# A planner's costs recounted in a four-layer graph network: landing times per kind of transfer, a microsecond in hand for each, and VectorE's pauses

## The chip, the cores and the metric

The kernel runs on one core of one Trainium2 chip. The metric is the device time of one execution in microseconds (us). Before the change the median of three runs is 2305.0 us (2304.22 to 2305.61). All arithmetic is in fp32.

## The reference

Thirty-two graphs of 512 nodes go through four layers. Each layer multiplies by the graph's 512 x 512 adjacency matrix, applies one or two dense products, adds the result to its input and normalises over the 256 features. The data of one graph never meets another's.

```python
def layernorm(x): return (x - mean(x)) / sqrt(var(x) + 1e-5)          # over the 256 features
# x: (32, 512, 256), adj: (32, 512, 512)
def L0(x): return relu(((1 + eps) * x + adj @ x) @ W1 + b1) @ W2 + b2     # 256 -> 512 -> 256
def L1(x): h = adj @ (x @ W.T + b); return where(h > 0, h, alpha * h)
def L2(x): h = layernorm(x); return x + relu((adj @ h) @ W_rel + b_rel + h @ W_root)
def L3(x):
    h = (epsilon * x + adj @ x) @ W1 + b1                                 # 256 -> 1024
    return silu(h * rsqrt(mean(h * h) + 1e-6) * rms_weight) @ W2 + b2     # 1024 -> 256
for L in (L0, L1, L2, L3):
    x = layernorm(x + L(x))
```

## The kernel before

**The work of a graph.** One graph's activations (512 x 256) fill one "room", an SBUF buffer of 128 partitions x 1024 floats; there are 36 rooms, and up to five graphs are under way at once (`FLIGHT`). An adjacency matrix fills two rooms and is loaded by four transfers of 256 KB; x is one transfer of 512 KB. Every large product is done as seven products of half size in place of eight, so VectorE makes many sums and differences of blocks before a product (`left_sums`, `right_sums`) and adds many PSUM results after it. ScalarE does the normalisations' sums and scalings, the activations and copies out of PSUM. GpSimd does only small powers (`inv_sqrt`).

**Transfers inside the core.** Where a tensor must be turned, VectorE transposes squares of 32 x 32 and SyncE's queue carries them through a buffer in device memory and back: four transfers of 128 KB out (`corner<-room` in the profile), then one of 512 KB or four of 128 KB back in (`room<-corner`). `spread_squares` and `gather_squares` do this in two layouts. The diagonal blocks of the adjacency are put aside and brought back in the same way (`diagonal`), and `everywhere` spreads one row over all partitions through `line`. `carry` moves four blocks from room to room, for the first graph alone.

**The order of the work.** The program's order is fixed when it is built. Each helper (`mm`, `add`, `copy`, `move` ...) only records an `Op` with, for each engine that could do it, a pair of times: how long the engine is busy, and how long after that the result is there. `Plan.order` then simulates the engines with these times and writes down the ops in the order in which they start; engines then run their own streams in this order, held only by semaphores. Line 332 issues nearly all compute instructions and line 372 all transfers.

What the simulation goes by:

- An op's **rank** is a due time: the graph's number times a period, plus a shift for single graphs (`SHIFT`), plus the TensorE work of its graph that lies before the product that needs it, times a pace, less the cost of the chain between (`needs`). `near` weighs that chain. The last three graphs (`LATE`) follow at a spacing of their own. Among ops that can start at the same moment on an engine, the lowest rank goes first. `RULES` holds period, pace, last spacing and `near`.
- `AHEAD` bounds how far, in units of rank, an op that takes a new room may be ahead of the foremost matmul that is still to do.
- A **transfer** occupies SyncE's queue for `ISSUE` and lands at the end of its turn on the wire (kbytes / 385) plus `ADVANCE` 1.5 us, plus `late` and `AFTER`. At most eight are under way (`LANES`). What reads the target can't start earlier in the simulation, and the room isn't free before.
- An op that both ScalarE and VectorE can do goes to VectorE only if it would end there `YIELD` us earlier.
- **Pauses.** A GpSimd power and VectorE instructions with two SBUF operands are kept apart (`port`). After VectorE has made a power's input, the next such instruction starts no earlier than `PORT` = 0.55 us later. If nothing else fits, the simulated idle time is stored as `op.pause`, and the emitter at line 1454 fills it with small memsets, one for each 0.11 us:

```python
if op.pause and op.way == "vector":
    for _ in range(round(op.pause / 0.11)):
        nc.vector.memset(pause, 0.0)
```

Of the kernel before, what the change touches and what calls it, by code (L numbers as in the profile page):

```python
# [14 lines left out]
P = 128  # L15
Q = 32
# [4 lines left out]
def span(ap):  # L21

    n = 1
    for d in ap.shape[1:]:
        n *= d
    return n
# [38 lines left out]

ISSUE, ADVANCE, AFTER, LANES = dict(sync=0.45, within=0.66, gpsimd=1.5), 1.5, 0.8, 8


def wire_time(kbytes):
    return kbytes / 385
# [19 lines left out]
SOON = 0.03  # L92


YIELD = 1.4

# [2 lines left out]

RULES = [(35, 1.8, 14, 0.8)]

SHIFT = {-2: -3, -1: -12}


AHEAD, LAST = 55.0, 500.0


TURN = {0: (99, 0), 2: (99, 0), 3: (0, 3)}
# [132 lines left out]
class Plan:  # L247
# [113 lines left out]
        ways = {"vector": ((busy, vector_time(1)[1]), issue)}  # L361
        self.add(ways, [s[0] for s in steps], ins, port=True, crosses=True)

    def move(self, out, src, kbytes, engine="sync", late=0.0, into=None, outof=(), **kw):


        within = engine == "sync" and isinstance(out, Part) and isinstance(src, Part)
        kind = "within" if within else engine

        def issue():  # L370
            to, of = (x.place() if isinstance(x, Part) else x for x in (out, src))
            getattr(self.nc, engine).dma_start(to, of, **kw)  # L372

        self.add(
            {engine: ((ISSUE[kind], ADVANCE + late + wire_time(kbytes) + AFTER), issue)},
            into or out, [*outof, *([src] if isinstance(src, Part) else [])],
            kbytes=kbytes, late=late,
        )
# [53 lines left out]
    def best(self):  # L432


        rule = min(RULES, key=lambda rule: self.order(*rule)[0])
        return self.order(*rule)[1]

    def order(self, period, pace, last, near):
# [4 lines left out]
        rank = [  # L443
            (min(op.graph, final) * period + max(op.graph - final, 0) * last + SHIFT.get(op.graph, 0) + SHIFT.get(op.graph - B, 0) + n, i)
            for i, (op, n) in enumerate(zip(self.ops, need))
# [11 lines left out]
        oldest, ahead, wire, lanes = 0, 0, 0.0, [0.0] * LANES  # L457
# [9 lines left out]
        while can_start:  # L467
# [50 lines left out]
            for i in can_start:  # L518
                op = self.ops[i]
# [6 lines left out]
                if op.kbytes and "sync" in op.ways:  # L526
# [4 lines left out]
                way = min(  # L531
                    at, key=lambda e: at[e] + sum(op.ways[e][0]) + YIELD * (op.yields and e == "vector")
                )
# [3 lines left out]
            t, engine = min((min(c)[0], e) for e, c in best.items())  # L537
            soon = t + (1e-6 if engine == "tensor" else SOON)
            _, t, i = min((r, s, i) for s, r, i in best[engine] if s <= soon)
            op = self.ops[i]  # L540
# [15 lines left out]
            end = t + busy + tail  # L556
# [6 lines left out]
                    port["vector"] = t + busy + PORT  # L563
            if op.kbytes:
                wire = max(wire, t + ADVANCE) + wire_time(op.kbytes)
                end = wire + op.late + AFTER
                if engine == "sync":
                    lanes = [*lanes[1:], end]
            for r in op.rooms:
# [27 lines left out]
def tile_gnn_stack(ctx: ExitStack, tc: tile.TileContext, a: dict, out: bass.AP):  # L597
# [26 lines left out]
    B, N, D = a["x"].shape  # L624
    NC = N // P
    DC = D // P
# [13 lines left out]
    plan = Plan(nc, FLIGHT)  # L640
# [31 lines left out]
    def vector(method, n, *args, **kw):  # L672
        return "vector", method, vector_time(n), args, kw

    def scalar(func, n, x, times=scalar_time, **kw):
        columns = sum(k in ("scale", "bias") and not isinstance(v, float) for k, v in kw.items())
        return "scalar", "activation", times(n, columns), (x,), dict(func=func, **kw)
# [34 lines left out]
        plan.do(o, way)  # L712

    def carry(o, x):
        plan.move(o, x, o.shape[0] * span(o) / 256, late=1.2)

    def inv_sqrt(o, x):
        n, p = span(o), o.shape[0]
# [5 lines left out]
    def room(*shape):  # L724
        return Part(Room(rooms)).shaped(*shape)
# [120 lines left out]
    class Adjacency:  # L846
# [35 lines left out]
        def restore(self):  # L882
            for i in range(4):
                if plan.graph == 0:
                    carry(self.loops[i], self.kept[:, i])
                elif i < 2:
                    for k in range(HC):
                        c = i * HC + k
                        block = a["adj"][plan.graph][:, c, c * P : (c + 1) * P]
                        plan.move(self.loops[i][:, k], block, P * P / 256)  # L890
                else:
                    name = f"{self.kept.tensor.name}{i}"
                    d = self.kept[:, i - 2]
                    plan.move(self.loops[i], d, P * HC * P / 256, outof=[name])
# [134 lines left out]
    def dense_turned(right, left, bias=None):  # L1029
# [27 lines left out]
        for k in range(DC):  # L1057
# [5 lines left out]
                ),  # L1063
            )
        y = spread_squares(squares)
        return y.whole(P // Q, NC, DC, Q).then(lambda v: v.rearrange("p a c k j -> p c k a j"))

# [34 lines left out]
    class Norm:  # L1102
# [44 lines left out]
        def put(self, c, y, scale, shift):  # L1147
            r = self.r[:, c, :]
            plan.do(
                y[:, c, :],  # L1150
                vector(
                    "tensor_scalar", D, r, self.less[:, c : c + 1], scale, op0=ALU.add, op1=ALU.mult
                ),
                scalar(AF.Identity, D, r, scale=scale, bias=shift),
            )
# [53 lines left out]
    def spread_squares(of):  # L1209

        to = room(P // Q, NC * DC * Q)
        of, via = of.whole(P // Q, NC * DC * Q), next(corners)
        names = [f"{via.tensor.name}{a}" for a in range(P // Q)]
        places = via.rearrange("(b i) (a x) -> a i b x", i=Q, a=P // Q)
        for a, name in enumerate(names):
            plan.move(places[a], of[a * Q : (a + 1) * Q], Q * N * DC / 256, into=name)
        plan.move(to.whole(N * DC), via, P * N * DC / 256, late=0.8, outof=names)
        return to  # L1220

    def gather_squares(to, of):

        to, of, via = to.whole(N * DC), of.whole(N * DC // Q, Q), next(corners)
        names = [f"{via.tensor.name}{a}" for a in range(P // Q)]
        via = via.rearrange("(i b) x -> i (b x)", i=Q)
        places = via.rearrange("i (m a j) -> a i m j", a=P // Q, j=Q)
        for a, name in enumerate(names):  # L1230
            plan.move(places[a], of[a * Q : (a + 1) * Q], Q * N * DC / 256, into=name)
        blocks = via.rearrange("i (b x) -> b i x", b=P // Q)
        for b in range(P // Q):
            plan.move(to[b * Q : (b + 1) * Q], blocks[b], Q * N * DC / 256, late=0.8, outof=names)

    def everywhere(sums, ops):

# [37 lines left out]
    def load_x(b):  # L1275
        x = tok()
        src = a["x"][b].rearrange("(p c) d -> p c d", c=NC)
        if b:
            plan.move(x, src, N * D / 256, late=1.6)
        else:  # L1280
            for h in range(2):
                plan.move(half(x, h), half(src, h), N * D / 512, late=1.6)
        return x

    def layer0(x, adjacency):
        adjacency.sums()
        adjacency.with_loops(loop0)
        aT = aggregate(x, adjacency)
        adjacency.restore()
        turn = turns(0)  # L1290
        if not turn:
            plus_row(x, b2_0)
        h1 = Wide(FC0)
        dense_feat(aT, A1_0, b1_0, h1, lambda f: act(h1.pair(f), h1.pair(f), AF.Relu))
        norm = Norm(x)
        right = dense_sums([halves(h1.pair(0))], [halves(h1.pair(2))])
        if turn:
            add_turned(x, dense_turned(right, A2_0, b2c_0), norm.half)
        else:
            dense_add(x, right, A2_0, norm.half)  # L1300
        norm.scales((1.0, LN_EPS))
        return norm.scaled()
# [104 lines left out]
    x = load_x(0)  # L1407
# [13 lines left out]
    x = layer0(x, adjacency)  # L1421
# [22 lines left out]
    for b in range(1, B):  # L1444
        plan.graph = b
        x, adjacency = load_x(b), Adjacency(b)
# [3 lines left out]
    with tc.manual_schedule():  # L1450
        for op in plan.best():
            if op.pause and op.way == "vector":
                for _ in range(round(op.pause / 0.11)):
                    nc.vector.memset(pause, 0.0)  # L1454
            op.ways[op.way][1]()

# [36 lines left out]
```

## Time and profile before

| | |
|---|---|
| median of three runs | 2305.0 us |
| profiled execution: its own time / span of its instructions | 2306.6 us / 2304.8 us |
| TensorE (PE) busy, 12434 matmul records | 2283.2 us, 99% |
| weight loads (PEld) busy | 2035.4 us, 88% |
| VectorE (DVE) busy, 5702 instructions | 2149.7 us, 93% |
| ScalarE (ACT) busy | 1667.8 us, 72% |
| GpSimd (POOL) busy, 168 instructions | 240.1 us, 10% |
| DMA moved / share of the 16 DMA engines' time | 167.73 MB / 25.6% |
| granted TensorE clock | 0.999 |

An fp32 matmul of the program is two MATMUL and two LDWEIGHTS records, so counts of matmuls below are of records. A busy PE is not a PE at its peak: a matmul's record lasts longer than the distance to the next one's start, so busy records overlap and a small stall between two of them doesn't show as idle time. Gaps under 0.15 us are not listed as idle. In a line of the timeline the columns are start, duration, engine, line of the kernel, operation, tiles and shapes, the number of merged instructions, and in square brackets the idle time before it with what ended it.

### The profile page before, as it was taken

The page shows a single profiled execution, that of the slowest core. Times are in us where ns is not written, and L with a number is a line of the kernel's source. Part 1 is how long each engine was busy: PE and PEld are TensorE (multiplying, and loading weights), DVE is VectorE, ACT ScalarE, POOL GpSimd, SP SyncE. Part 2 cuts the span into 40 slices and gives each one's busy share as a digit, 9 for nine tenths or more (in the row PEclk, how much of TensorE's full clock was granted, in tenths as well). Part 3 has the DMA queues.
Part 4 walks back from the last instruction along what each step waited for, and adds up shares of the span by engine and source line. Part 5 has one row for each costly group of instructions (what it writes and reads, how often), then busy time and mean ns, then how long its engine had stood idle before and what let it go on. Part 6 is the DMA issues. An engine that isn't in the chain of part 4 may idle for free.

```text
span 2304.8 us, 38247 instructions
## 1 busy us (share of the span) xinstructions
PE 2283.2 (99%) x12434; PEld 2035.4 (88%) x12434; DVE 2149.7 (93%) x5702; ACT 1667.8 (72%) x4509; POOL 240.1 (10%) x168
## 2 busy tenths in 40 slices
PE   9999999999999999999999999999999999999998
PEld 7889898888888888888988888888888888988987
DVE  8999899989999999999999999999999999989898
ACT  4776678767777767777777776768767777678685
POOL 0001101111101111101110011110111101101011
PEclk9999999999999999999999999999999999999999
DMA  7111323123212233222332122221323212222201
GB/s 215 49 27 32 80 72 86 46 85 86 80 50 79 74 91 85 58 61 74 92 85 65 53 83 83 85 69 49 91 75 86 81 49 79 74 69 70 64 6 69
DMA packets 244584, 167.73 MB, mean 73 GB/s; under 512 B 141856, under 2 KB 207648, under 8 KB 244384
## 3 DMA queue, kind: packets, MB, share of 16 engines
q1 hardware_dynamic: 244384, 165.29, 25.2%
q8 instruction: 98, 1.61, 0.3%
q14 instruction: 102, 0.84, 0.1%
HBM read 109.33 MB, written 55.37 MB: 71 GB/s over the span
## 4 chain that ended last, share of the span: by engine, by line
PE 87%; DVE 6%; DMA 3%; ACT 2%; SPq 1%; issue 1%; ACTq 0%; DVEq 0%
PE ps L332 87%; DVE room L332 5%; DMA room<-in_adj_dram 2%; ACT room L332 1%; ACT scrap L332 1%; SPq L372 1%; DMA room<-corner 0%; DMA corner<-room 0%; DVE few L332 0%; DMA room<-in_x_dram 0%; DVE few L351 0%; DVE A L332 0%; ACTq L1489 0%; DVE pause L1454 0%; DVE shift L332 0%
## 5 line engine op out<-in xcount | busy, mean ns | idle before, releaser
L332 PE MATMUL ps<-room,room 128*128 128x256 f32 x3584 | 928.0, 381 | 2.7 <-DMA room<-in_x_dram 2.3
L332 DVE TENSOR_TENSOR room<-room,room 128x512 f32<-128x512 f32 (+1 forms) x1416 | 808.3, 595 | 21.2 <-ACT room L332 11.0
L332 PEld LDWEIGHTS ps<-room,room 128*128 128x128 f32 x3584 | 649.7, 191 | 89.3 <-ACT room L332 8.3
L332 PE MATMUL ps<-room,L_gnn_W 128*128 128x256 f32 x2432 | 677.9, 382 | 1.3 <-DVE room L332 1.1
L332 DVE TENSOR_TENSOR room<-ps,room 128x256 f32<-128x256 f32 (+1 forms) x1232 | 555.6, 477 | 15.5 <-PE ps L332 10.2
L332 PE MATMUL ps<-room,A 128*128 128x256 f32 x1824 | 514.1, 380 | 0.6 <-ACT room L332 0.6
L332 PEld LDWEIGHTS ps<-room,L_gnn_W 128*128 128x128 f32 x2432 | 440.9, 191 | 66.4 <-DVE room L332 18.3
L332 ACT ACTIVATE room<-ps,L_gnn_b_c 128x256 f32<-128x256 f32 x880 | 364.3, 468 | 138.7 <-PE ps L332 136.5
L332 POOL TENSOR_TENSOR few<-few,mhalf 128x4 f32<-128x4 f32 (+3 forms) x162 | 239.4, 1479 | 2056.6 <-DVE few L332 1161.8
L332 ACT ACTIVATE room<-room,few 128x256 f32<-128x256 f32 x593 | 315.5, 593 | 84.8 <-DVE few L332 80.4
L332 PEld LDWEIGHTS ps<-room,A 128*128 128x128 f32 x1824 | 333.6, 191 | 42.1 <-ACT room L332 1.3
L332 PE MATMUL ps<-L_gnn_W,room 128*128 128x128 f32 (+1 forms) x1792 | 346.2, 305 | 1.4 <-DVE room L332 1.4
L332 DVE TENSOR_TENSOR room<-room 128x256 f32<-128x256 f32 (+1 forms) x640 | 313.7, 497 | 30.4 <-DMA room<-corner 21.5
L332 PEld LDWEIGHTS ps<-L_gnn_W,room 128*128 128x128 f32 x1792 | 295.1, 191 | 28.9 <-DVE room L332 1.8
L332 ACT ACTIVATE scrap<-room 128x256 f32<-128x256 f32 x500 | 204.5, 410 | 136.3 <-DVE room L332 130.5
L332 ACT ACTIVATE room<-room 128x1024 f32<-128x1024 f32 (+2 forms) x260 | 243.7, 938 | 69.9 <-DVE room L332 60.0
L332 ACT ACTIVATE scrap<-room,few 128x256 f32<-128x256 f32 x500 | 250.3, 501 | 58.4 <-DVE few L332 54.7
L332 ACT ACTIVATE room<-ps 128x256 f32<-128x256 f32 x516 | 190.1, 375 | 131.3 <-PE ps L332 130.5
L332 PE MATMUL ps<-A,room 128*128 128x128 f32 x1728 | 269.1, 276 | 2.5 <-DVE room L332 2.3
L332 PEld LDWEIGHTS ps<-A,room 128*128 128x128 f32 x1728 | 250.0, 192 | 19.4 <-DVE room L332 5.7
L332 ACT ACTIVATE room<-room,L_gnn_rms_weight_c 128x512 f32<-128x512 f32 x256 | 175.6, 716 | 11.7 <-DVE room L332 11.6
L332 DVE TENSOR_TENSOR room<-room,loop 128x256 f32<-128x256 f32 x256 | 103.4, 407 | 38.3 <-PE ps L332 37.0
(60 smaller groups left out, 1181.0 us busy)
## 6 DMA issues: line engine op xcount, KB each, us to landing
room<-in_adj_dram SPq DMA_DIRECT2D x128, 256.0 KB, 5.0
corner<-room SPq DMA_DIRECT2D x232, 128.0 KB, 2.7
room<-in_x_dram SPq DMA_DIRECT2D x31, 512.0 KB, 6.5
room<-corner SPq DMA_DIRECT2D x120, 128.0 KB, 2.7
out_dram<-room SPq DMA_DIRECT2D x30, 512.0 KB, 3.0
room<-corner SPq DMA_DIRECT2D x28, 512.0 KB, 3.6
diagonal<-room SPq DMA_DIRECT2D x62, 128.0 KB, 1.8
room<-in_adj_dram SPq DMA_DIRECT2D x124, 64.0 KB, 2.0
```

The costliest lines, as they stand in the source:

```text
L332: getattr(getattr(self.nc, engine), method)(to, *(put(x) for x in args), **kw)
L372: getattr(self.nc, engine).dma_start(to, of, **kw)
```

## The change

The numbers that the simulation goes by are set anew, transfers get a margin, and the number of memsets in a pause is counted by another formula. No instruction of the computation is added or removed; the order, the engine of an op that has two, and the number of memsets may differ.

- `ISSUE` of an ordinary transfer 0.45 to 0.48 us; `gather_squares` gives its four outgoing transfers 0.7.
- `AFTER` 0.8 to 0.4, and in the simulation every landing is put off by `SPARE` = 1.0. In the chain costs for the due times `KEEP` = 0.4 is added instead, so these stay at 0.8 in all.
- `late` per kind: outgoing turned squares 0 to 0.1 (spread) and 0.3 (gather); coming back 0.8 to 0.4; `carry` 1.2 to 0; loads of x and adjacency stay at 1.6, `line` and its way back stay at 0 and 0.8.
- `YIELD` 1.4 to 1.6; period 35 to 34; spacing of the last graphs 14 to 11; `near` 0.8 to 0.4; `SHIFT` from -3 (last but one) and -12 (last) to -21 (last), +3 (second graph) and +6 (third); `AHEAD` 55 to 85.
- Memsets of a pause: `round(pause / 0.11)` to `round((pause + 0.115) / 0.175)`.

```diff
-ISSUE, ADVANCE, AFTER, LANES = dict(sync=0.45, within=0.66, gpsimd=1.5), 1.5, 0.8, 8
+ISSUE, ADVANCE, AFTER, LANES = dict(sync=0.48, within=0.66, gpsimd=1.5), 1.5, 0.4, 8
+SPARE = 1.0
+KEEP = 0.4
...
-YIELD = 1.4
+YIELD = 1.6
...
-RULES = [(35, 1.8, 14, 0.8)]
-SHIFT = {-2: -3, -1: -12}
-AHEAD, LAST = 55.0, 500.0
+RULES = [(34, 1.8, 11, 0.4)]
+SHIFT = {-1: -21, 1: 3, 2: 6}
+AHEAD, LAST = 85.0, 500.0
...
-    def move(self, out, src, kbytes, engine="sync", late=0.0, into=None, outof=(), **kw):
+    def move(self, out, src, kbytes, engine="sync", late=0.0, into=None, outof=(), issue=None, **kw):
...
-            {engine: ((ISSUE[kind], ADVANCE + late + wire_time(kbytes) + AFTER), issue)},
+            {engine: ((issue or ISSUE[kind], ADVANCE + late + wire_time(kbytes) + AFTER + KEEP), put)},
...
             if op.kbytes:
                 wire = max(wire, t + ADVANCE) + wire_time(op.kbytes)
-                end = wire + op.late + AFTER
+                end = wire + op.late + AFTER + SPARE
...
     def carry(o, x):
-        plan.move(o, x, o.shape[0] * span(o) / 256, late=1.2)
+        plan.move(o, x, o.shape[0] * span(o) / 256)
...
     def spread_squares(of):
-            plan.move(places[a], of[a * Q : (a + 1) * Q], Q * N * DC / 256, into=name)
-        plan.move(to.whole(N * DC), via, P * N * DC / 256, late=0.8, outof=names)
+            plan.move(places[a], of[a * Q : (a + 1) * Q], Q * N * DC / 256, late=0.1, into=name)
+        plan.move(to.whole(N * DC), via, P * N * DC / 256, late=0.4, outof=names)
...
     def gather_squares(to, of):
-            plan.move(places[a], of[a * Q : (a + 1) * Q], Q * N * DC / 256, into=name)
+            plan.move(
+                places[a], of[a * Q : (a + 1) * Q], Q * N * DC / 256, late=0.3, into=name, issue=0.7
+            )
...
-            plan.move(to[b * Q : (b + 1) * Q], blocks[b], Q * N * DC / 256, late=0.8, outof=names)
+            plan.move(to[b * Q : (b + 1) * Q], blocks[b], Q * N * DC / 256, late=0.4, outof=names)
...
             if op.pause and op.way == "vector":
-                for _ in range(round(op.pause / 0.11)):
+                for _ in range(round((op.pause + 0.115) / 0.175)):
                     nc.vector.memset(pause, 0.0)
```

More of the change, by code (lines that the diff above doesn't have):

```diff
@@ L362, in row, with put @@
         self.add(ways, [s[0] for s in steps], ins, port=True, crosses=True)
-    def move(self, out, src, kbytes, engine="sync", late=0.0, into=None, outof=(), **kw):
+    def move(self, out, src, kbytes, engine="sync", late=0.0, into=None, outof=(), issue=None, **kw):
         within = engine == "sync" and isinstance(out, Part) and isinstance(src, Part)
         kind = "within" if within else engine
-        def issue():
+        def put():
             to, of = (x.place() if isinstance(x, Part) else x for x in (out, src))
```

## The prediction

> **What bounds the kernel now.** I read the page first: its busy shares.
>
> ```profile
> PE 2283.2 (99%) x12434; PEld 2035.4 (88%) x12434; DVE 2149.7 (93%) x5702; ACT 1667.8 (72%) x4509; POOL 240.1 (10%) x168
> ```
>
> TensorE never stops for long, so I priced a PE without stalls. Long merged runs in the timeline give the distance between matmul starts: twenty 128x256 records in 4.48 us, (4.48 - 0.38) / 19 = 0.216 us; thirty-eight 128x128 records in 4.41 us, (4.41 - 0.28) / 37 = 0.112 us. The groups, kept apart by shape, hold 8378 records of the first kind and 4056 of the second: 1809.6 + 454.3 = 2263.9 us. The first starts at 1.2 and the last ends at 2294.6 (timeline), then 10.2 us pass to the end of the span. 1.2 + 2263.9 + stalls + 10.2 = 2304.8 leaves **29.5 us of stalls**; with the change, PE's work stays the same, so only these and the two ends can move.
>
> Going through the starts in the timeline: about 6.6 us of them lie before 50 us (first loads and weights), 2.7 up to 150, 2.8 up to 480, 15.0 between 480 and 2050, 2.5 after. The middle is periodic: the chain shows a graph every 71.13 us, 22 periods, 0.68 us lost in each. Two patterns make most of that.
>
> First, the pause. VectorE's timeline, then TensorE's:
>
> ```profile
> 1225.65 0.23 DVE L332 TENSOR_SCALAR few<-few 128x4 f32<-128x4 f32 x2
> 1225.83 0.80 DVE L1454 MEMSET pause<- 128x48 f32 x5
> 1226.55 1.24 DVE L332 TENSOR_TENSOR room<-room,room 128x512 f32<-128x512 f32 x2
> ...
> 1229.32 0.41 DVE L332 TENSOR_TENSOR room<-ps,room 128x256 f32<-128x256 f32 x1
> ```
>
> ```profile
> 1229.29 0.60 PE L332 MATMUL ps<-room,A 128*128 128x256 f32 x2
> 1229.79 0.70 PE L332 MATMUL ps<-room,L_gnn_W 128*128 128x256 f32 x2
> 1230.32 0.60 PE L332 MATMUL ps<-room,A 128*128 128x256 f32 x2
> ```
>
> Two such records should take 0.43 us. The pair at 1229.29 takes 0.50: the next waits 0.06 to 0.07 us for VectorE's add of 1229.32. After each such stop the following distance is 0.10 longer as well (1229.79 to 1230.32 is 0.53). VectorE runs without a gap from the pause to this add, so it is late by what the pause took too long. The same recurs at 1234.4. In the middle I find 42 such stops, two a period: 2.7 us, and 4.4 us in the distances behind them, 7.0 in all.
>
> Second, the adjacency. The chain, in order of time:
>
> ```profile
> 1188.97 6.07 DMA room<-in_adj_dram
> ...
> 1195.13 0.69 DVE room L332
> 1195.83 0.18 DVE few L332 x2
> 1196.00 1.10 DVE room L332 x3
> ...
> 1197.17 0.42 DVE room L332
> 1197.59 0.04 issue
> 1197.63 71.14 PE ps L332 x380
> ```
>
> The load took 6.07 us to land; the simulation allows 1.5 + 0.66 + 1.6 + 0.8 = 4.57. VectorE stood waiting for it with all its later work behind, and 2.5 us on PE stood too. Of this sort I find 12 stops in the middle, 3.8 us with 1.2 behind them, 5.0 in all. The waits agree on who is late:
>
> ```profile
> PEld ps L332 <- DVE room L332: 29.6, 94, 1.5
> DVE room L332 <- DMA room<-corner: 21.5, 15, 5.6
> DVE room L332 <- DMA room<-in_adj_dram: 8.8, 12, 1.8
> ```
>
> [...] the trace has a median of 5.0 and up to 7.5 for the adjacency[...], and it is the scatter that a margin is for.
>
> **The change part by part.**
>
> *Memsets.* 361 of 98 ns; five take 0.80 us, so they start (0.80 - 0.098) / 4 = 0.175 us apart. A pause of five was planned as 0.495 to 0.605 us, since it is rounded in steps of 0.11, and holds VectorE for 5 x 0.175 - 0.115 = 0.76 by the new formula's own account (0.67 from the end of 1225.88 to 1226.55). New: (0.495 to 0.605 + 0.115) / 0.175 rounds to 4 (3 only at the very edge); three (0.275 to 0.385) become 2 or 3. I count 52 fives and 24 threes, so about 52 + 12 memsets go, 11 us of VectorE, which costs nothing by itself: VectorE has gaps. A pause under 0.055 us, which got none, now gets one, 0.06 us of delay. What counts is that 0.175 us goes per pause of five, more than the 0.06 to 0.07 that PE waits: if the order stayed, the 7.0 us would go whole. GpSimd's power starts 0.1 to 0.2 us after its input, well inside four memsets, so the shorter pause shouldn't cost there.
>
> *Landings in the simulation.* Adjacency: 4.57 becomes 0.66 + 1.5 + 1.6 + 0.4 + 1.0 = 5.17 (+0.6; median measured 5.0). x: 5.23 to 5.83 (measured 6.5, still short). Outgoing corners: 2.63 to 3.33 and 3.53 (measured 2.7). Coming back: 3.43 to 3.63 for 128 KB, 4.43 to 4.63 for 512 KB (measured 2.7 and 3.6). In the middle VectorE waits nine times for the adjacency, 0.7 us on average; 0.6 covers a little over half of it: 3 of the 5.0 us. Corner waits cost PE about 3.5 us (at 256, 470 and 2084 us), and at least one landing there took over 6 us: 1 us back. `carry`, in the first graph only, goes the wrong way: 3.83 to 3.23 planned, 4.1 measured; its four results are used 0.5 to 1.1 us after landing, so it may cost 0 to 1 us once.
>
> *Queues.* Issues cost SyncE what they did; only their place moves. `AHEAD` lets five loads a graph (five issues of 0.4 us) go up to 30 / 1.8 = 17 us of PE work earlier, if rooms are free. On SyncE they stand ahead of corner and diagonal moves, and a load that waits for its room holds those up. In the simulation they go only when the room is free, so I take nothing; the bound is in the slower rival.
>
> *YIELD.* At most the 47 scalings that VectorE took (0.37 us each) go to ScalarE, which has 28% free. Nothing.
>
> *Period, `near`, the shifts.* They reorder everything. `near` 0.4 makes long chains ahead of a product more urgent, which should lengthen PE's lead. Head and tail: 1.2 + about 9 us at the start, 10.2 at the end; the trace can't price a new order, I bound it by -3 and +4 and take 0.
>
> *New near misses.* Any other order has ops that are ready just as PE wants them. The old one lost 15 us in the middle with pauses 0.2 us too long and landings 0.6 short; with both mended I let 3.5 us come back. Sum: -7.0 - 3 - 1 + 3.5 = -7.5: 2304.8 becomes 2297.3. The runs' median lies 0.2 above the profiled span: **2297.5 us**.
>
> **Rivals.** *The order eats it:* near misses come back at other places, as many as before. For it: 0.7 us a period is only six stops of 0.06 plus 0.1. Against it: both patterns have a cause that the change takes away. 2304, within 2300.4 to 2309.6 (0.2%, about what a measurement of this kernel can tell from no change).
>
> *Rooms run short, slower:* early loads take three of 36 rooms up to 17 us sooner, and targets are held 0.2 to 0.9 us longer in the plan; some room that a product's result needs comes free later, and the same gap opens every period. Its price is that of the worst stop in the middle now, 1.07 + 0.10 us at 1053.8. For it: the four adjacency loads at 1044.1 go out back to back when rooms come free, 9 us before their use, so rooms are scarce; SyncE's waits for VectorE to let go of rooms sum to 1061 us. Against: the simulation counts rooms. At 1.0 us in each of 27 periods, less the 11 gained: 2304.8 + 27 - 11 = 2321. It decides from 11 / 27 = 0.4 us a period on.
>
> *The pauses alone work,* margins are lost in the new order: -7 + 3.5, 2301.5; it belongs to "same".
>
> **How the numbers follow.** Forecast (own range 2289 to 2300.4): 0.52. No net change, with the pauses alone: 0.20. Rooms or another periodic gap: 0.28, of which half ends above 2318. The forecast's lower bound takes all 15 us of the middle and 3 of the tail: 2287. Faster 0.53, same 0.20, slower 0.27; range 2287 to 2318.
>
> **What would show it.** Pauses of four memsets, not five, and no 0.06 us stop of layer 1's dense matmuls behind them. VectorE's waits for the adjacency below 8.8 us. The chain's period at 70.6 to 70.9 in place of 71.13. I am wrong if the period is longer than 71.13: then its largest repeated stop names the cause. If it is shorter and the time still not, head or tail took it: PE's last matmul to the end of the span over 10.2, or over 9 us lost before 150.

## The result and the profile after

The changed kernel takes 2285.68 us (median of four runs, 2285.43 to 2285.75), the kernel before 2305.31 us beside it: a ratio of 0.991, 95% interval 0.9898 to 0.9922. It is faster by about 19.6 us, where 7.5 were forecast; the time lies 1.3 us below the range. The profiled span went from 2304.8 to 2283.9 us.

The busy shares of the kernel after:

```profile
PE 2268.7 (99%) x12434; PEld 2044.5 (90%) x12434; DVE 2132.9 (93%) x5471; ACT 1693.8 (74%) x4551; POOL 241.1 (11%) x168
```

The matmuls are the same 12434. VectorE has 231 instructions fewer: 189 memsets (361 in pauses before, 172 after) and 42 scalings, which ScalarE took (42 more).

The last matmul now ends at 2272.8 us in place of 2294.6, so with the same 2263.9 us of matmuls at their pitch the stalls fell from 29.5 to about 7.7 us. By stretch: 9.3 to 7.2 before 150 us (the stops up to 50 us, at the first loads and weights, stay), 2.8 to 0.4 up to 480, 15.0 to 0.8 between 480 and 2050, 2.5 to 1.8 after that. (These sum to a little more, 10.2: 0.216 is rounded up by some 0.3 ns, which is 2.5 us over 8378 records. The same count gives 30.8 for the kernel before, so the prediction's list, 29.6, had left out about 1 us.) From the last matmul to the end it is 11.1 us, 0.9 more than before.

The period is read from GpSimd's timeline, from one power of a graph's layer to the next graph's:

```profile
1211.82 1.64 POOL L337 TENSOR_TENSOR few<-few,mhalf 128x8 f32<-128x8 f32 x1 [14.71 <-DVE few L337]
...
1282.16 1.64 POOL L337 TENSOR_TENSOR few<-few,mhalf 128x8 f32<-128x8 f32 x1 [14.71 <-DVE few L337]
```

It is 70.34 us, where the chain before showed 71.13, and just below the 70.6 to 70.9 that the prediction named. Who waits for whom in the kernel after (who, for what: us in total, times, longest):

```profile
DVE room L337 <- PE ps L337: 91.0, 149, 2.5
...
PEld ps L337 <- DVE room L337: 3.7, 8, 1.5
...
DVE room L337 <- DMA room<-in_adj_dram: 2.2, 2, 1.2
```

TensorE's weight loads waited 94 times for VectorE, now 8 times. VectorE's 15 waits for turned squares (21.5 us) are gone from the list, those for the adjacency are down from 12 to 2. In place of these VectorE waits for TensorE, 91.0 us where it was 48.4. The stretch that the prediction showed now looks like this, first VectorE, then TensorE:

```profile
1211.50 0.24 DVE L337 TENSOR_SCALAR few<-few 128x4 f32<-128x4 f32 x2
1212.10 0.42 DVE L337 TENSOR_TENSOR room<-ps,room 128x256 f32<-128x256 f32 x1 [0.36 <-PE ps L337]
1212.44 0.68 DVE L337 TENSOR_TENSOR room<-room,L_gnn_b 128x512 f32<-128x512 f32 x1
```

```profile
1211.90 0.59 PE L337 MATMUL ps<-room,L_gnn_W 128*128 128x256 f32 x2
1212.33 1.46 PE L337 MATMUL ps<-room,room 128*128 128x256 f32 x6
1213.62 0.60 PE L337 MATMUL ps<-room,A 128*128 128x256 f32 x2
```

There is no pause at all: an add that reads PSUM stands behind the power's input, and it waits 0.36 us for TensorE. TensorE's starts are 0.43 us for two and 1.29 for six, the pitch and no more.

For the comparisons below one line of the windows view serves as a common measure: the stretch from 480 to 2050 us of each kernel, with the matmul records in it in the first bracket. Before, then after:

```profile
480.00:2050.00 1570.00, 1568.08 (x8394) 1391.73 (x8393) 1470.44 (x3918) 1158.18 (x3153) 167.01 (x111) 1.00 0.26 75
```

```profile
480.00:2050.00 1570.00, 1569.82 (x8465) 1414.39 (x8464) 1473.61 (x3752) 1189.62 (x3208) 165.72 (x111) 1.00 0.27 75
```

71 matmuls more in the same time are 71 x 70.34 / 388.6 = 12.9 us of work, against the 14.2 us that the count of starts gives. PE's busy time hardly moves, the weight loads' does. "The middle" below is this stretch, and its loss is counted from the starts of matmuls as in the prediction. The last graphs begin after 1950, so a loss "up to 1950" is counted from 480 and is that of the periodic part alone: about 14.8 us before, none after.

### The profile page after: what moved, and what is told of

The parts are those of the page before. It is cut to its first block, busy times and chain, and to the rows that moved or that the text cites. A ratio compares the mean times of both kernels' runs of the same rounds, so it can differ in the third digit from the quotient of the medians.

```text
span 2283.9 us, 38000 instructions
## 1 busy us (share of the span) xinstructions
PE 2268.7 (99%) x12434; PEld 2044.5 (90%) x12434; DVE 2132.9 (93%) x5471; ACT 1693.8 (74%) x4551; POOL 241.1 (11%) x168
## 5 line engine op out<-in xcount | busy, mean ns | idle before, releaser
L337 PE MATMUL ps<-room,room 128*128 128x256 f32 x3584 | 940.9, 380 | 1.6 <-DMA room<-in_x_dram 1.2
L337 PE MATMUL ps<-room,L_gnn_W 128*128 128x256 f32 x2432 | 654.4, 380 | 1.4 <-DVE room L337 1.1
L337 DVE TENSOR_TENSOR room<-ps,room 128x256 f32<-128x256 f32 (+1 forms) x1232 | 568.2, 479 | 85.2 <-PE ps L337 78.2
L337 ACT ACTIVATE room<-room,few 128x256 f32<-128x256 f32 x635 | 335.0, 591 | 60.8 <-DVE few L337 60.6
L337 PEld LDWEIGHTS ps<-room,A 128*128 128x128 f32 x1824 | 326.1, 191 | 35.4 <-ACT room L337 0.9
L337 DVE TENSOR_TENSOR room<-room 128x256 f32<-128x256 f32 (+1 forms) x640 | 307.7, 495 | 4.4 <-ACT room L337 1.9
L337 ACT ACTIVATE room<-ps 128x256 f32<-128x256 f32 (+1 forms) x516 | 194.2, 378 | 153.5 <-PE ps L337 147.4
L337 PEld LDWEIGHTS ps<-A,room 128*128 128x128 f32 x1728 | 258.8, 191 | 17.7
```

The lines of the kernel that those rows point to most:

```text
L337: getattr(getattr(self.nc, engine), method)(to, *(put(x) for x in args), **kw)
```

## The experiments

My theory after the result: wrong costs in the simulation made the stops, late landings more than I had priced; the pauses' share and the landings' share can be had one at a time. The rival: the new rules (period, `near`, `AHEAD`, shifts) give TensorE its lead, whatever the costs. Times below are given as ratios to the kernel before on the same chip, since the medians of that kernel differ from chip to chip: 2306.1 us on the chip of pause_only, 2304.6 on that of spare_only, 2303.8 on that of loads_margin.

**The pauses alone.**

```diff
 # before, and
-                for _ in range(round(op.pause / 0.11)):
+                for _ in range(round((op.pause + 0.115) / 0.175)):
```

> Before, with the new count of memsets and nothing else; the order is that of before. If the pauses' excess made the two stops a period in layer 1 (7.0 us in the middle), these vanish and the adjacency's stay: 2298 us (2296 to 2300). If VectorE's lag has other sources and the order alone matters (rival): 2303 to 2306, stops still there.

Measured: 0.9987 (0.9981 to 0.9994), 2303.2 against 2306.1 us: 2.9 us, not 7. The middle's loss is 10.1 us in place of 15.0 (the start loses about 1 us more), and of the 42 stops in layer 1 there are 23 left: they cost 4.2 us where it was 7.0. The other 2 us or so come off the stops behind the adjacency. VectorE and TensorE at the same place as in the prediction:

```profile
1223.71 0.62 DVE L1454 MEMSET pause<- 128x48 f32 x4
1224.25 1.24 DVE L332 TENSOR_TENSOR room<-room,room 128x512 f32<-128x512 f32 x2
```

```profile
1229.76 0.59 PE L332 MATMUL ps<-room,L_gnn_W 128*128 128x256 f32 x2
1230.19 0.59 PE L332 MATMUL ps<-room,A 128*128 128x256 f32 x2
...
1231.91 1.22 PE L332 MATMUL ps<-room,L_gnn_W 128*128 128x256 f32 x4
1232.97 0.38 PE L332 MATMUL ps<-room,A 128*128 128x256 f32 x1
```

Four memsets, as foreseen. The first stop is gone, the second is as it was: four records should take 4 x 0.216 = 0.86 us, and from 1231.91 to 1232.97 it is 1.06. This shows the error. VectorE has no gap from the pause to both adds, so its lag is one. The first stop (0.07 + 0.10) puts TensorE back by 0.17, then it is late enough and doesn't stop again until VectorE has fallen behind anew. Taking 0.175 us from the pause moves both adds by 0.175; TensorE, which no longer stops the first time, comes 0.17 earlier to the second, and waits there as before. From the stop behind the adjacency to this second stop TensorE takes 36.93 us (1195.50 to 1232.43) where it took 37.10 (1197.63 to 1234.73): one relief, not two. I had counted it twice. (A second pause of five stands in that stretch. What it gave back, VectorE lost again in two gaps around 1218.7, 0.18 us.)

**Landing times and margin alone.**

```diff
 # after, with the old pauses and the old rules
+YIELD = 1.4
+RULES = [(35, 1.8, 14, 0.8)]
+SHIFT = {-2: -3, -1: -12}
+AHEAD, LAST = 55.0, 500.0
+                for _ in range(round(op.pause / 0.11)):
```

> Before with the transfers' new issue and landing times and the microsecond in hand, old pauses, old rules, shifts, AHEAD and YIELD. If late landings made their own stops (5.0 us in the middle, 3.5 elsewhere) these vanish and the pauses' stops stay: 2297 us (2294 to 2301). Rival, that period, near and AHEAD give PE its lead: 2301 to 2308.

Measured: 0.9957 (0.9945 to 0.997), 2295.6 us. The middle's loss is down to 1.5 us, the pauses' stops included, although the pauses are counted in the old way; the order puts 146 memsets in place of 361. The loss moved to the ends: 11.3 us before 150 and 9.9 after 1950.

**The rules alone.**

```diff
 # before, and
-YIELD = 1.4
+YIELD = 1.6
-RULES = [(35, 1.8, 14, 0.8)]
+RULES = [(34, 1.8, 11, 0.4)]
-SHIFT = {-2: -3, -1: -12}
+SHIFT = {-1: -21, 1: 3, 2: 6}
-AHEAD, LAST = 55.0, 500.0
+AHEAD, LAST = 85.0, 500.0
```

> Before with the new period, near, last spacing, shifts, AHEAD and YIELD, old landing times and old pauses. If the stops come from wrong costs: 2300 to 2308, with stops behind pauses and behind late landings. Rival, that these rules give PE its lead whatever the costs: 2285 to 2291.

Measured: 0.9995 (0.9987 to 1.0004): no difference in the whole. The middle still loses 13.5 us, but elsewhere than before: up to 1950 it is 7.5 us in place of 14.8, with seven stops in layer 1 in place of 42, and between 1950 and 2050 it is 6.1 in place of 0.4. The end after the last matmul is 1.4 us longer too. So the rival falls for the time as a whole and not for the periodic part: under the old costs the new rules clear half of that, and lose about as much where the last graphs begin and at the end.

**Landing times, margin and pauses, with the old rules.**

```diff
 # landing_only, and
-                for _ in range(round(op.pause / 0.11)):
+                for _ in range(round((op.pause + 0.115) / 0.175)):
```

> Landing times, margin and the new count of memsets, with the old period, near, last spacing, shifts, AHEAD and YIELD. The landing times alone left no stop between 500 and 1950 us, so a shorter pause has nothing to take away there: 2293.5 to 2296. Rival, that the gains of the two parts add up: 2291 to 2293.

Measured: 0.9946 (0.9933 to 0.9959), 2294.5 us, one microsecond below landing_only, but the intervals overlap, so no difference is shown. The middle loses 1.5 us in both: there the shorter pause has nothing left to return. Whether the gains add up over the whole run these times can't tell, since 0.9987 times 0.9957 would be 0.9944.

**After, with the old pauses.**

```diff
 # after, and
-                for _ in range(round((op.pause + 0.115) / 0.175)):
+                for _ in range(round(op.pause / 0.11)):
```

> After, with the old count of memsets; the order is that of after. If the new order still has products that follow VectorE closely, the old pauses bring stops back: 2289 to 2293. Rival, that the new order gives PE so much lead that 0.2 us on VectorE don't reach it: 2285 to 2287.

Measured: 0.993 (0.9917 to 0.9942), 2289.2 us, 3.5 above the kernel after. The middle has 21 stops of 0.10 us, one a period, and 3.5 us of loss in all. So the new order's lead at its tightest place is smaller than the 0.2 us that an old pause takes too long.

**The margin alone.** The times per kind, pauses and rules of before:

```diff
-                end = wire + op.late + AFTER
+                end = wire + op.late + AFTER + 1.0
```

> Before with one edit: every landing in the simulation is put off by 1.0 us; old times per kind, old pauses, old rules. If the margin alone clears the middle: 2294 to 2299, with VectorE's waits for transfers in the middle near zero. Rival, that the times per kind are needed: 2301 to 2312.

Measured: 0.9957 (0.9944 to 0.9969), 2294.8 us, the same as landing_only. This one edit takes the middle's loss from 15.0 to 5.0 us, of which 3.0 are two stops after 2000, where the last graphs begin. The middle, and VectorE's wait for turned squares in it:

```profile
480.00:2050.00 1570.00, 1567.52 (x8441) 1405.34 (x8439) 1462.59 (x3752) 1177.35 (x3208) 168.31 (x112) 1.00 0.27 75
```

```profile
DVE room L332 <- DMA room<-corner: 1.1, 3, 0.5
```

It was 13.1 us in 12 waits in the same stretch before. The time doesn't show whether the new times per kind add anything to the margin; up to 1950 the loss is 1.4 us here and 0.1 in landing_only.

The margin doesn't only move landings. It makes another order, and that order leaves fewer pauses to fill: 194 memsets in place of 361 under the old formula. The stops of layer 1 cost 1.4 us up to 1950 in place of 7.0. So pauses and landings can't be taken apart cleanly.

**Whose margin.** Two complements of the last edit: loads of x and adjacency alone (they are marked by `late` 1.6), and all other transfers.

```diff
 # loads_margin                                         # moves_margin: 0.0 if ... else 1.0
-                end = wire + op.late + AFTER
+                end = wire + op.late + AFTER + (1.0 if op.late == 1.6 else 0.0)
```

> Before with 1.0 us in hand for the loads of x and adjacency alone. If late adjacency loads are the cause of their own stops only: these 5.0 us go, the two stops a period in layer 1 stay: about 2300 plus what the ends change (2297 to 2303). Rival, that the loads' lateness is behind all stops of the middle: no stop there, 2290 to 2297.

> The complement: before with 1.0 us in hand for all transfers but the loads of x and adjacency. If late turned squares put VectorE behind in layer 1: the two stops a period go (7.0 us), the adjacency's stay: 2296 to 2301. Rival, that these transfers cost PE only the 3.5 us seen: 2301 to 2306.

Measured: loads_margin 1.002 (1.0014 to 1.0027), 2308.6 us; moves_margin 0.9974 (0.9963 to 0.9984), 2298.6 us. Their middles:

```profile
480.00:2050.00 1570.00, 1568.38 (x8408) 1396.04 (x8408) 1471.66 (x3976) 1167.15 (x3181) 171.72 (x111) 1.00 0.27 75
```

```profile
480.00:2050.00 1570.00, 1569.69 (x8424) 1395.39 (x8424) 1475.89 (x3931) 1157.32 (x3164) 165.91 (x111) 1.00 0.27 75
```

TensorE starts 8394 records in it before, 8408 and 8424 here. The middle's loss is 12.1 with the loads' margin and 7.6 with the others'. The loads' margin saves 2.9 us there, the others' 7.4; both together 10.0 (spare_only). That this adds up is chance. Up to 1950 the halves save about 3.6 and 7.4 and the whole 13.3, and in the whole run they bring +4.9 and -5.2 us where both together bring -9.8. loads_margin is slower in all because its last graphs lose 7 us after 2150. Nor does each half clear its own stops. The loads' margin takes the adjacency's stops from 5.3 us to 0.4, but stops at other products grow by about 4. The others' margin takes 3.4 us from the adjacency's stops and 2.9 from layer 1. Neither half clears layer 1: of the 42 stops 31 and 22 are left. Each edit makes another order, so what an edit brings is not the share of one cause. Which of the other transfers matter (turned squares, diagonals, the row) was not tried.

**After, without and with half the margin.**

```diff
-SPARE = 1.0
+SPARE = 0.0        # after_no_spare
+SPARE = 0.5        # after_spare05
```

> After without the microsecond in hand: landings planned by the new times per kind alone (the adjacency at 4.17 us, below the 5.0 measured). If the margin is what cleared the middle, stops behind late landings return: 2290 to 2300. Rival, that the new times per kind and the new rules suffice: 2284 to 2288.

> After with half the margin (0.5): the adjacency is planned to land at 4.67 us, still below the 5.0 measured, turned squares at 2.83 to 3.03, above the 2.6. If the margin has to reach the adjacency's median, stops return, a good part of the 139 us that no margin cost: 2300 to 2400. Rival, that any margin does: 2284 to 2290.

Measured: without margin 1.0514 (1.0497 to 1.0531), 2424.6 us; with half of it 0.9948 (0.9935 to 0.996), 2291.9 us. I expected a few microseconds in the first case; it is 139 above the kernel after. Half the margin clears the stretch up to 1950 as well as the whole does, so the plan need not reach the adjacency's median (4.67 planned, 5.0 measured). What it loses against 1.0 lies where the last graphs begin and after, 5.7 us of it between 1950 and 2000. The chain of the kernel without margin, at one of its stops:

```profile
1107.27 5.10 DMA room<-in_adj_dram
...
1112.39 0.69 DVE room L337
...
1114.21 0.24 DVE room L337
1114.46 4.54 DMA diagonal<-room
1119.00 0.02 issue
1119.02 0.43 DVE room L337
1119.46 0.04 issue
1119.50 45.58 PE ps L337 x214
```

A load that is planned at 4.17 us lands after 5.10. VectorE's sums of its blocks are late, with them the move that puts the diagonal aside, and that one takes 4.54 us to land where 2.23 were planned, while loads and turned squares are on the way beside it. VectorE must not change the diagonal before, so TensorE stands for 3.4 us. One landing that was planned too early is followed by a second in the same chain. The run has 23 such stops of TensorE, 77 us in all, and some 40 us go behind them at a lower clock: the mean granted clock is 0.981, where it is 0.999 in the kernel after, and 0.018 of 2429.8 us is 44 (last section). The times per kind fit the medians of the turned squares, 2.33 and 2.53 us planned on the way out against 2.6 measured, but not the adjacency's, 4.17 against 5.0. The new rules over the old times, with the adjacency at 4.57, had one such stop, of 2.4 us, and took 2305.1 us (rules_only).

**The old AHEAD.**

```diff
-AHEAD, LAST = 85.0, 500.0
+AHEAD, LAST = 55.0, 500.0
```

> After with the old AHEAD of 55. If loads that go early are part of the gain, loads land later before their use and PE stops more often: 2295 to 2315. Rival, that AHEAD only mattered at the start: 2285 to 2289.

Measured: 1.0018 (1.001 to 1.0025), 2308.9 us. The middle is as clean as in the kernel after. What is lost lies behind 2050: 16 us up to 2100, mostly in two waits for ScalarE, 14.6 us together, 2.6 up to 2150 and 6.1 after 2250. The longer wait:

```profile
PEld ps L337 <- ACT room L337: 9.0, 1, 9.0
```

So both answers that I had written down are wrong: earlier loads are no part of the gain in the middle, and the start doesn't need them either; the last graphs do.

**The start and `near`.**

```diff
-SHIFT = {-1: -21, 1: 3, 2: 6}
+SHIFT = {-1: -21}                      # after_no_head
-RULES = [(34, 1.8, 11, 0.4)]
+RULES = [(34, 1.8, 11, 0.8)]           # after_near08
```

> After without the shifts of the second and third graph (+3, +6). If these cleared the stretch from 50 to 150 us: 2288 to 2294 with 4 to 5 us of stalls there. Rival, that near and the period did: 2285 to 2287.

> After with near back at 0.8. If near gave the lead at the start or in the middle: over 2290, with stalls there. Rival, that it only reorders: 2284 to 2288.

Measured: 0.9942 (0.9929 to 0.9954), 2291.3 us, and 0.9989 (0.9982 to 0.9995), 2301.5 us. Without the shifts of the second and third graph TensorE loses 5.7 us between 50 and 150 in place of 0.4: they cleared the start. With `near` at 0.8 the start is clean, but 3.4 us go between 350 and 550 and 13 after 2200. The shifts are tied to the start, `near` mostly to the last graphs.

**The last graphs.**

```diff
-RULES = [(34, 1.8, 11, 0.4)]
-SHIFT = {-1: -21, 1: 3, 2: 6}
+RULES = [(34, 1.8, 14, 0.4)]           # after_old_tail
+SHIFT = {-2: -3, -1: -12, 1: 3, 2: 6}
+RULES = [(34, 1.8, 13, 0.4)]           # after_tail13
+SHIFT = {-1: -12, 1: 3, 2: 6}
```

> After with the old spacing of the last graphs (14) and their old shifts (-3, -12); period, near, AHEAD, YIELD and the shifts of the second and third graph stay new. With the landing times alone PE lost 7.5 us after 2200 us. If the new last spacing and shifts mended that: 2289 to 2294, with the loss after 2100. Rival, that near, AHEAD and the first graphs' shifts gave the rest: 2284 to 2287.

> After with last spacing 13 and shifts -12 (last), +3, +6: between the tail of after and the old tail, which was 1.7 us faster. If PE's stalls of 3.3 us after 2250 in the old tail go while its shorter end of 7.5 us stays: 2281 to 2283.5. If the two trade against each other: 2284 to 2287.

Measured: 0.99 (0.9886 to 0.9914), 2284.0 us, and 0.9917 (0.9904 to 0.9931), 2285.6 us. With the old spacing TensorE loses 3.3 us after 2250, but from its last matmul to the end it takes 7.5 us in place of 11.1. With 13 there is no loss after 2250, and the end takes 12.2. The two trade. after_old_tail is the fastest version run, by 1.7 us, but its interval and that of the kernel after overlap and they were not run side by side, so I don't call it shown.

**No pauses at all.**

```diff
 # before, and
-                for _ in range(round(op.pause / 0.11)):
+                for _ in range(0):
```

> Before with no memset in any pause, same order. If pauses only cost time, VectorE gains 0.4 to 0.8 us at each and PE's stops behind them go: 2297 to 2302. Rival, that GpSimd's power is then held up by VectorE's two-operand instructions and its readers are late: over 2309.

Measured: 1.0008 (1.0 to 1.0017), 2309.2 us. The 361 memsets are gone and the kernel isn't faster. GpSimd's line of before, then GpSimd's and VectorE's without the pause, in the same place:

```profile
1225.96 1.64 POOL L332 TENSOR_TENSOR few<-few,mhalf 128x8 f32<-128x8 f32 x1 [16.26 <-DVE pause L1454]
```

```profile
1225.87 2.94 POOL L332 TENSOR_TENSOR few<-few,mhalf 128x8 f32<-128x8 f32 x1 [16.22 <-DVE few L332]
```

```profile
1228.85 0.24 DVE L332 TENSOR_TENSOR few<-few 128x4 f32<-128x4 f32 x2 [0.73 <-POOL few L332]
```

The same power takes 2.94 us in place of 1.64, and VectorE, which goes on 0.76 us sooner (0.14 us from the start of 1225.56 to the next work at 1225.70, 0.90 before), waits 0.73 us for it. What VectorE gains it gives back at the reader of the power.

## Why the prediction was wrong

The direction and three of the signs held: pauses of four, no periodic stop of layer 1, adjacency waits below 8.8 us. The size failed. Pauses and landings were put at -11 us together and brought 12.5 (landing_pause), but that agreement is luck: the pauses were priced too high and the landings too low. The rest of the gap lies in two terms, 3.5 us of new near misses that did not come, and about 8 us from the rules, which I had put at nothing. The steps one by one:

- *Memsets.* "The 7.0 us would go whole" is wrong. One lag of VectorE makes both stops of a period, and its relief pays for one. Alone it took 2.8 us from the stops of layer 1, 5.0 from the middle and 2.9 from the whole run.
- *Landings.* I gave the margin 3 us for the adjacency and 1 us for turned squares. Alone it brought 10.0 us in the middle and 9.8 in all (spare_only). I had priced each late landing by the stop just behind it, in the old order, and put the stops of layer 1 down to the pause alone. But new landing times make a new order, in which these stops went from 7.0 to 1.4 us up to 1950. The 3 us agree with loads_margin (2.9) by luck: the adjacency's own stops lost 4.9 us there and others came. For the 1 us, moves_margin has 7.4. How the margin of these other transfers acts stays open. A likely guess, that VectorE's waits for squares (13.1 us in the middle) stay in its lag until TensorE stops in layer 1, does not hold in the trace of before. After each of the eleven longer waits up to 1700 VectorE stands idle for TensorE, at least once for 0.3 to 1.2 us, before TensorE's next stop for it, so the lag is gone by then. One of them:

```profile
1032.51 0.69 DVE L332 TENSOR_TENSOR room<-room 128x512 f32<-128x512 f32 x1 [1.45 <-DMA room<-corner]
...
1042.43 0.42 DVE L332 TENSOR_TENSOR room<-room,loop 128x256 f32<-128x256 f32 x1 [0.48 <-PE ps L332]
```

- *New near misses.* The 3.5 us that I let come back did not: 0.8 us are left in the middle. I had counted the new order as a loss, and it is where much of the gain lies: in the kernel after VectorE comes to its products first and waits for TensorE.
- *Period, near, the shifts.* "I take 0", with -3 and +4 as bounds. On top of landings and pauses they bring about 8 us (0.9946 to 0.991): TensorE's loss before 150 goes from 11.3 to 7.2, after 1950 from 9.4 to 2.2, the end grows from 7.5 to 11.1. It is mainly a repair: the new costs under the old rules lose more at both ends than the kernel before did. Against the kernel before, the start brings 2.1 and the last graphs about 1 us, less the 0.9 at the very end. The new rules with the margin alone, without the times per kind, were not run.
- *The lower end.* 2287 took 15 us of the middle and 3 of the tail and left out the 5.5 us that my own list had between 50 and 480; 4.6 of these went.
- *YIELD* as nothing: 42 scalings moved to ScalarE. It was not run alone, so that it is worth nothing is not shown.
- *Rivals.* Rooms did not run short: the period is shorter, and no stop is left between 480 and 1950. That the order eats the gain is refuted by the result, and that the pauses alone work by spare_only.

## What to carry to other kernels

Where one engine is the bound and others feed it in order, keep something in hand on the landing times of a plan: a plan that let loads land 0.8 us before their median cost 139 us here, and one with half a microsecond in hand, still 0.3 us before that median, lost nothing in the steady state. Count one lag once, however many stops it makes. When costs in a planner change, the order changes with them, so the stops of the old order don't give the price; and settings tied to the start and the end have to be set again.

## What the runs showed of the hardware

- A GpSimd power of 128x8 takes 1.64 us behind a pause and, without pauses, 2.94 us beside VectorE instructions with two SBUF operands (21 of 32 powers in no_memsets, where VectorE's waits for powers come to 17.4 us in 25 waits, against one of 1.2 in the kernel before). The start makes the difference in these traces: all 21 began while such an instruction ran. Of the 324 powers of before and after six began so, and these alone are longer: five of 128x4 take 1.43 to 2.28 us where the others take 1.01, one of 128x8 takes 1.8. Where such an instruction begins later, for 54 of the 64 powers of 128x8 in before and after 0.4 to 0.6 us behind the power's start (1225.96 and 1226.55 in the prediction's stretch), the power still takes 1.64. Powers of 32x16 take 2.89 there.
- After a stop of 3.42 us TensorE ran at half its clock for some six microseconds (0.50 granted from 1119 to 1125, 1.00 from 1126 to 1136). Its timeline and the clock (third last number of the window) in the kernel without margin:

```profile
1119.50 6.59 PE L337 MATMUL ps<-room,room 128*128 128x256 f32 x16 [3.42 <-DVE room L337]
1125.93 1.03 PE L337 MATMUL ps<-room,L_gnn_W 128*128 128x256 f32 x4
```

```profile
1119.00:1125.00 6.00, 5.50 (x13) 4.42 (x14) 4.41 (x10) 2.47 (x5) 0.00 (x0) 0.50 0.19 60
```

  The starts of the sixteen records span 6.43 us where 16 x 0.216 = 3.46 are due: the stop costs almost twice its length (3.42 + 2.97 us). The length alone does not decide it in this run: of its 23 stops, idle for 2.6 to 3.8 us, at 19 the clock is halved behind the stop, the shortest of 2.63 among them, and at four it is not, one of them of 3.50.
- Behind each of the 42 stops of layer 1 in the kernel before, the next pair starts 0.10 us late as well, so a wait of 0.06 us costs 0.17. The tail is as long, 0.10 us, behind the stops for the adjacency, which go up to 1.07 us. Other short stops, mostly of 0.05 or 0.10 us and put down to no engine, have none.
